# A planned two-layer transformer kernel on one core: weighted values by unit instead of by pair, a one-instruction spread of masked values, one-instruction query scaling, and a newly searched order

## The chip, the cores and the metric

The kernel runs on one core of a Trainium2 chip, as one launch. The metric is the device time of that launch in microseconds, the median of several executions. Times of the profile come from one profiled execution.

## The reference, and what must be computed

Sixteen sequences of 256 tokens with 128 features go through four stages, each followed by a residual and a layer norm. All numbers are 32-bit floats.

```python
x = ln(x + attention(x, Wq, Wkv, Wo, bo))                 # 16 heads of 64, softmax over 256 keys
x = ln(x + routed_ffn(x, signatures, ...))                # a tile of 64 chosen per token, then a tiny spline net
x = ln(x + gate * linear_attn(ln(x)) + (1 - gate) * window_attn(ln(x)) ...)   # window of 65 keys, 16 heads of 8
x = ln(x + moe(causal_qk_norm_attention(ln(x))))          # 16 heads of 64, causal; then 8 experts, all run, 128 -> 512 -> 128
```

Two of the four stages hold an attention with 16 heads of 64. For each head the weights are `softmax(q k^T)` over 256 keys (causal in the second one), and the head's output is `weights @ v`. In the causal attention q and k are divided by their norm and multiplied by a learned scale per feature. The window attention has 16 heads of 8 features; its values `h @ wv_loc + bv_loc` are needed head by head.

## The kernel before: tiling, stages, and who sets the order

**Work units.** The 16 sequences form `NG = 8` groups of two (512 tokens). Every group goes through stages a (first attention), b (routed net), c (linear and window attention), d (causal attention) and e (experts). Within a stage a or d a sequence is worked in *units* of four heads, a unit being two *pairs* of two heads (64 + 64 features fill 128 partitions).

**A pair** (`pair`, from L643) issues: the scores of both heads (64 rows by 128 columns of the array, mode "r", L662 on); a masking add in the causal case (L669); negated row maxima (L678, L688); two exponentials with row sums per head (L707); a reciprocal (L714); a scaling on GpSimd (L720); a transpose of the weights on TensorE into PSUM (L735) and its copy to a `pt` tile on VectorE or ScalarE (L587, L585). Then the weights meet the values, `values`, in a mode of 128 rows by 64 columns ("c64"), so that two heads run side by side into one PSUM bank of which a pair uses 256 columns, and one copy of 128x256 takes the result to an `ov` tile. Four `ov` tiles, one a pair, are multiplied into the width of the model by `into_width`.

**The window attention** (stage c) works in 64 blocks of 64 queries (8 groups, 2 sequences, 4 blocks). Its values are spread into four copies, each zero except for one of every four heads (tiles `vm`, three of them, [128, 4, 128]), by four VectorE additions a block of 4 x 8 columns each (`spread`, L1128). The product with `vm` runs in mode "c32" (128 rows by 32 columns).

**The causal queries** (stage d, `keep`, L1289 on ScalarE, L1291 on VectorE): the projected queries of a unit stand in one PSUM bank of 512 columns, 256 a pair; each pair is scaled by its own column of `qks`, in an instruction of its own, which the planner may give to VectorE or ScalarE.

**Experts** (stage e): per expert four "up" products (128x512, L579), four Gelu activations (L1433), sixteen "down" products in four accumulations, and four accumulating VectorE instructions (L1449). The weights `w1` and `w2` of every expert (256 KB each) are loaded by SyncE's queue again for every group (L1420, L1423), into a pool of two tiles each.

**The order is planned.** No engine's order is written by hand. Every piece above is a task (`W.add`) with allowed engines, a cost in ns, the buffers that it reads, writes or holds, and a due time: `due(g, stage) = g * PACE[stage] + OFF[stage]`, in units of a group. Before the program is emitted, `Plan.line` walks through a list schedule with its own costs: it always takes the task that can begin first, ties broken by due time. Buffers come from the pools of `SLOTS` (class, columns, count); four PSUM banks ("p") and two double banks ("s") are fixed. `SHIFTS` is a list of seeds; each one adds a random disturbance to the due times of some tasks, and the list is what a search kept. The program is then emitted in that order, and each engine runs its own instructions in order and waits on semaphores. When tasks of another array mode follow each other the planner reckons with a drain (`DRAIN`, `CHANGE`), and with 1300 ns when ScalarE changes its function table (`SWITCH`). The Gelus of `NBURST = 2` experts are a *burst*: once ScalarE has begun one, it takes nothing else until the burst is done.

Of the kernel before, what the change touches and what calls it, by code (L numbers as in the profile page):

```python
# [19 lines left out]
P = 128  # L20
# [7 lines left out]
QC = 64  # L28
# [7 lines left out]
NX = 5  # L36
NBURST = 2

OFF = {"a": 0.116, "b": 1.829, "c": 2.055, "d": 3.635, "e": 5.316}
PACE = {"a": 0.877, "b": 0.855, "c": 0.892, "d": 0.951, "e": 0.997}  # L40


def due(g, stage):
# [3 lines left out]

SLOTS = (
    ("x", 512, 5),
    ("xT", 512, 2),  # L50
    ("ua", 512, 5),
    ("uq", 512, 4),
    ("ud", 512, 4),
    ("pb", 512, 5),
    ("pt", 512, 5),
    ("ov", 256, 7),
    ("m", 64, 18),
    ("k1", 256, 6),
    ("b", 512, 2),
    ("sc", 288, 1),  # L60
    ("c", 512, 6),
    ("vl", 516, 1),
    ("qm", 512, 1),
    ("pbC", 512, 2),
    ("ptC", 512, 3),
    ("d", 512, 3),
    ("h2", 512, 1),
    ("kn", 512, 2),
    ("sq", 512, 2),
    ("e", 512, 1),  # L70
    ("hid", 512, 6),
    ("w1", 512, 2),
    ("w2", 512, 2),
)

# [26 lines left out]
class Plan:  # L102
# [11 lines left out]


    SHIFTS = (
        342893, 622819, 786828, 493542, 1031372, 82152, 761358, 224577, 886183, 799202, 814949, 920728, 485348,
        97950, 792974, 882706, 644055, 901515, 175912, 740398, 460392, 490772, 219754, 766672, 812234, 385264,
        789951, 343118, 300004, 391487, 87697, 604865, 1032146, 998679, 152137, 764351, 457160, 307203, 582915,
        594534, 694184, 860491, 449845, 535977, 830298, 828009, 821526, 248210, 581561, 551500, 161509, 113298,  # L120
        555122, 883686, 415166, 991453, 344589, 404904, 418158, 370246, 601370, 461514, 823304, 25842, 794354,
        915253, 557407, 471164, 404291, 181653, 172993, 113307, 463275, 910893, 228032, 531592, 575482, 539031,
        84463, 349997, 228975, 77199, 436200, 405493, 989484, 4908, 562557, 73629, 962183, 941096, 638556,
        301435, 941950, 50702, 302818, 746995, 428703, 741343, 563752, 593640, 707837, 189096, 580269, 586128,
        882519, 591742, 638991, 205226, 680625, 626345, 1043368, 975522, 58852, 258028, 483328, 694436, 909676,
        241425, 473674, 1020055, 78442, 359882, 670620, 772336, 80084, 741629, 7155, 470604, 868845, 984347,
        1018080, 1031109, 71709, 237942, 360624, 360862, 1000988, 139054, 901420, 822374, 801430, 585138,
        797439, 64477, 369282, 125845, 898084, 716005, 751543, 409421,
    )

    def __init__(self, slots):
# [170 lines left out]
def kernel(ctx: ExitStack, tc: tile.TileContext, a: dict, out: bass.AP):  # L302
# [229 lines left out]
    hm = ctile("hm", [P, WH])  # L532

    NVM = 3
    vms = [ctile(f"vm{i}", [P, 4, D]) for i in range(NVM)]

    hsum = ctile("hsum", [P, 2, 32])
    cmask = ctile("cmask", [P, P])
# [97 lines left out]
        else:  # L636
            W.add("V", dve(512), lambda: nc.vector.tensor_scalar(o(), tp(), scale, shift, ALU.mult, ALU.add), r=[tp], w=[o])

    def pair(pi, qT, kT, v, ov, causal, rq, un=0):

# [51 lines left out]
        for par in range(2):  # L695
# [44 lines left out]
            W.add("P", 40 + pe(P, count=ncol // P, passes=1), turn, r=[pb], w=[tps, chain[1]], hold=[pt])  # L740
            W.add("VS", (dve(ncol), scl(ncol)), lambda e, pt=pt, tps=tps: copy(e, pt()[:, :ncol], tps()[:, :ncol]), r=[tps], w=[pt])
            pts.append(pt)
        ops = W.buf("p", "ops")

        def values():
            vv = v("p (k n) -> p k n", k=2)
            for kc in range(2):
                q0 = P if causal and kc else 0
                for par in range(2):
                    hc = slice((2 * pi + par) * DH, (2 * pi + par + 1) * DH)  # L750
                    mm(
                        ops()[par * DH : (par + 1) * DH, q0:S],
                        vv[:, kc, hc],
                        pts[par]()[:, kc * S : kc * S + S - q0],
                        start=kc == 0,
                        stop=kc == 1,
                    )

        W.add("P", pe(ncol, cols=0), values, r=[v] + pts, w=[ops, chain[2]], hold=[ov], mode="c64")
        W.add("VS", (dve(256), scl(256)), lambda e: copy(e, ov(), ops()[:, :S]), r=[ops], w=[ov])  # L760

    def into_width(ovs, w, hf, o, name):

        ps = W.buf("p", "po" + name)
        for qc in range(2):
            def go(qc=qc):
                for i in range(4):
                    mm(
                        ps()[:, qc * P : (qc + 1) * P], ovs[i]()[:, qc * P : (qc + 1) * P], w[:, 4 * hf + i, :],
                        start=i == 0, stop=i == 3,  # L770
                    )

            W.add("P", pe(P, count=4), go, r=ovs, w=[(ps, qc)])
        o(ps)


    def stage_a(g):
# [12 lines left out]
        def unit(b, p2):  # L790

            W.at = base + (4 * b + p2) / 8
            qT, kT, v = W.buf("ua", "qTA"), W.buf("ua", "kTA"), W.buf("ua", "vA")
            ps_q, ps_k, ps_v = W.buf("p", "psq"), W.buf("p", "psk"), W.buf("p", "psv")
            for dst, ps, w, scale in ((qT, ps_q, wq, DH**-0.5), (kT, ps_k, wkv, None)):

                def proj(ps=ps, w=w):
                    for i in range(2):
                        p = 2 * p2 + i
                        mm(ps()[:, i * S : (i + 1) * S], w[:, p * P : (p + 1) * P], xT()[:, b * S : (b + 1) * S])  # L800

                W.add("P", pe(S, count=2), proj, r=[xT], w=[ps], hold=[dst])

                def keep(e, ps=ps, dst=dst, scale=scale):
                    if scale is None:
                        copy(e, dst(), ps())
                    elif e == "S":
                        nc.scalar.mul(dst(), ps(), scale)
                    else:
                        nc.vector.tensor_scalar(dst(), ps(), scale, None, ALU.mult)  # L810

                W.add("SV", (scl(512), dve(512)), keep, r=[ps], w=[dst])

            def proj_v():
                for kc in range(2):
                    c0 = H * DH + p2 * 256
                    mm(ps_v()[:, kc * 256 : (kc + 1) * 256], xT()[:, b * S + kc * P : b * S + (kc + 1) * P], wkv[:, c0 : c0 + 256])

            W.add("P", pe(256, count=2), proj_v, r=[xT], w=[ps_v], hold=[v])
            W.add("SV", (scl(512), dve(512)), lambda e: copy(e, v(), ps_v()), r=[ps_v], w=[v])  # L820
            got = []
            for i in range(2):
                W.at = base + (4 * b + p2 + (i + 1) / 3) / 8
                ov = W.buf("ov", "ovA")
                pair(i, qT, kT, v, ov, False, None)
                got.append(ov)
            return got

        def seq(b):
            for hf in range(2):  # L830
# [184 lines left out]
    def stage_c(g):  # L1015
# [51 lines left out]
        for b in range(2):  # L1067
# [35 lines left out]
            for i, (w0, w1_) in enumerate(win_of):  # L1103
# [19 lines left out]
                W.add("P", pe(P), lambda pvw=pvw, w0=w0, w1_=w1_, nk=nk, b=b: mm(pvw()[:nk, :D], hT()[:, b * S + w0 : b * S + w1_], wvw), r=[hT], w=[pvw, vt])  # L1123

                def spread(pvw=pvw, vm=vm, nk=nk):
                    for l in range(4):
                        own = lambda t: t.rearrange("p (g e) -> p g e", e=4 * WD)[:, :, l * WD : (l + 1) * WD]
                        V.tensor_tensor(out=own(vm[:nk, l, :]), in0=own(pvw()[:nk, :D]), in1=own(bvw[:nk, :]), op=ALU.add)  # L1128

                W.add("V", 394, spread, r=[pvw], w=[vt])  # L1130
                sps = W.buf("s", "spsC")

                def scores(sps=sps, qm=qm, w0=w0, w1_=w1_, nk=nk, b=b):
# [48 lines left out]
                def values(po=po, pts=pts, vm=vm, nk=nk):  # L1182

                    for l in range(4):
                        for j in range(4):
                            r = slice(32 * j, 32 * j + 32)
                            h = 4 * j + l
                            c = ((h // 2) % 4) * P + (h % 2) * QC
                            mm(po()[r, :QC], vm[:nk, l, r], pts[j // 2]()[:nk, c : c + QC], start=l == 0, stop=l == 3)

                W.add("P", 600, values, r=[vt] + pts, w=[po, chain_c[2]], hold=[winT], mode="c32")
                W.add(
# [52 lines left out]
    def stage_d(g):  # L1245
# [9 lines left out]
        def half(b, hf):  # L1255
# [13 lines left out]
            for u in range(2):  # L1269
# [10 lines left out]
                squared = object()  # L1280
                W.add("S", scl(512), lambda sq_q=sq_q, ps_q=ps_q: act(sq_q(), ps_q(), AF.Square), r=[ps_q], w=[sq_q, squared])

                for i in range(2):

                    def keep(e, ps_q=ps_q, qT=qT, u=u, i=i):
                        p = 2 * (2 * hf + u) + i
                        c, o = qks[:, p : p + 1], slice(i * S, (i + 1) * S)
                        if e == "S":
                            A.mul(qT()[:, o], ps_q()[:, o], c)  # L1289
                        else:  # L1290
                            V.tensor_scalar(qT()[:, o], ps_q()[:, o], c, None, ALU.mult)  # L1291

                    W.add("VS", (391, 357), keep, r=[ps_q, squared], w=[(qT, i)])
            pq, nT, pn = W.buf("p", "pq"), W.buf("k1", "nT"), W.buf("p", "pnT")

            def norms():
# [34 lines left out]
            for u in range(2):  # L1331
# [20 lines left out]

                W.add("P", pe(P, count=4, passes=1), turn, r=[kn], w=[tps], hold=[kT])
                W.add("SV", (scl(512), dve(512)), lambda e, kT=kT, tps=tps: copy(e, kT(), tps()), r=[tps], w=[kT])
                for i in range(2):
                    W.at = base + (4 * b + 2 * hf + u + (i + 1) / 3) / 8
                    ov = W.buf("ov", "ovD")
                    pair(i, qTs[u], kT, v, ov, True, rqk, u)
                    got.append(ov)
            return got  # L1360

        def seq(b):
# [148 lines left out]
```

## Time and profile before

| what | value |
|---|---|
| time, median of 3 executions | 2079.08 us (2076.2 to 2080.76) |
| the profiled execution's own time | 2078.85 us |
| its span, first to last instruction | 2077.1 us |
| mean granted TensorE clock | 0.994 |
| ScalarE, copies `ov` of 128x256 | 107, mean 381 ns |
| VectorE, copies `ov` of 128x256 | 149, mean 416 ns |
| VectorE, spread additions | 256, 29.9 us busy in all |
| ScalarE / VectorE, query scalings of 128x256 | 89 of 507 ns / 39 of 478 ns |
| first and last matmul | begin at 5.5 us, end at 2064.9 us |

In the profile, PE is the matmul pipe, PEld its weight loads, DVE is VectorE, ACT ScalarE, POOL GpSimd, SP SyncE. A 32-bit matmul is two passes in the records (a transpose is one), so 9602 matmul instructions are 16394 records. The end of a matmul's record is modelled and lies behind the start of its successor, so the pitch from start to start tells what a matmul costs, not the record's length.

### The profile page before, as it was taken

The numbers are of one execution on the slowest core, as the hardware profiler recorded it, in microseconds if no ns is written. First come the engines' busy times: TensorE is split into PE (matmuls) and PEld (weight loads), VectorE is DVE, ScalarE is ACT, GpSimd is POOL, SyncE is SP. The second block draws the span as 40 slices with busy tenths as digits, with TensorE's granted clock in tenths as the row PEclk, the third lists the DMA queues.
The fourth block names the chain that finished last, engine by engine and source line by source line (L and its number), as shares of the span: only waits on it lengthen the run. The fifth ranks groups of instructions, "written<-read, shape, count | busy, mean of one in ns | idle before, by whom it ended". The sixth has DMA issues, their size and how long they took to land.

```text
span 2077.1 us, 46271 instructions
## 1 busy us (share of the span) xinstructions
PE 2007.3 (97%) x16394; PEld 1524.6 (73%) x16394; DVE 1583.7 (76%) x4843; ACT 1328.9 (64%) x4329; POOL 906.4 (44%) x1552
## 2 busy tenths in 40 slices
PE   8999999999999999999999999999999999999987
PEld 6777777776777777767777777777776776777755
DVE  6888989899936999469994599976897597485442
ACT  3556667777746776567775577763775587486542
POOL 4435565556505545146552265542463263152131
PEclk9999999999999999999999999999999999999989
DMA  6200000000011000110001100001001100100101
GB/s 137 47 1 1 2 2 1 2 2 1 2 57 31 7 1 2 51 33 12 2 2 33 50 12 2 2 21 45 19 7 36 47 7 22 52 16 26 57 21 51
DMA packets 69526, 47.74 MB, mean 23 GB/s; under 512 B 12112, under 2 KB 59952, under 8 KB 69296
## 3 DMA queue, kind: packets, MB, share of 16 engines
q1 hardware_dynamic: 68720, 43.74, 7.7%
q8 instruction: 130, 2.13, 0.4%
q10 hardware_dynamic: 576, 1.05, 0.2%
q14 instruction: 100, 0.82, 0.1%
HBM read 41.89 MB, written 2.88 MB: 22 GB/s over the span
## 4 chain that ended last, share of the span: by engine, by line
PE 60%; DVE 29%; ACT 5%; POOL 3%; issue 2%; DMA 0%; POOLq 0%; DVEq 0%; ACTq 0%; SPq 0%
PE p L579 43%; PE s L579 8%; PE p L735 5%; ACT pb L707 3%; DVE m L678 3%; DVE pt L587 2%; DVE m L688 2%; DVE s L669 2%; PE p L1175 2%; DVE s L1146 1%; DVE m L1151 1%; DVE x L617 1%; DVE m L1324 1%; DVE m L601 1%; PE p L1349 1%
## 5 line engine op out<-in xcount | busy, mean ns | idle before, releaser
L720 POOL TENSOR_SCALAR pb<-pb,m 128x256 f32<-128x256 f32 (+1 forms) x1024 | 461.6, 466 | 560.8 <-DVE m L714 491.4
L1433 ACT ACTIVATE hid<-p,b 128x512 f32<-128x512 f32 x256 | 173.3, 687 | 317.2 <-PE p L579 313.0
L707 ACT ACTIVATE pb<-s,m 128x256 f32<-128x256 f32 x512 | 237.4, 486 | 78.9 <-DVE m L688 71.3
L735 PE MATMUL p<-ident,pb 128*128 128x128 f32 x1792 | 267.5, 279 | 8.3 <-POOL pb L720 2.2
L707 ACT ACTIVATE pb<-s,m,m 128x128 f32<-128x128 f32 (+1 forms) x512 | 256.4, 524 | 22.7 <-DVE m L684 20.2
L579 PEld LDWEIGHTS p<-w,hid 128*128 128x128 f32 x2048 | 239.5, 192 | 25.9 <-issue 20.6
L735 PEld LDWEIGHTS p<-ident,pb 128*128 128x128 f32 x1792 | 201.4, 141 | 76.9 <-POOL pb L720 37.6
L579 PE MATMUL p<-w,hid 128*128 128x128 f32 x2048 | 243.1, 276 | 0.8 <-ACT hid L1433 0.2
L579 PE MATMUL p<-h,w 128*128 128x512 f32 x512 | 240.1, 605 | 0.1
L1449 DVE SCALAR_TENSOR_TENSOR e<-p,m,e 128x128 f32<-128x128 f32 x256 | 74.6, 344 | 206.1 <-PE p L579 155.3
L1169 POOL TENSOR_TENSOR pbC<-pbC,m 128x384 f32<-128x384 f32 (+1 forms) x128 | 119.7, 939 | 166.3 <-DVE m L1165 117.4
L1161 ACT ACTIVATE pbC<-s,m 128x96 f32<-128x96 f32 (+1 forms) x512 | 174.1, 376 | 8.5 <-DVE m L1151 5.4
L587 DVE COPY pt<-p 128x512 f32<-128x512 f32 (+1 forms) x258 | 156.8, 618 | 28.1 <-PE p L735 27.5
L585 ACT COPY pt<-p 128x384 f32<-128x384 f32 (+1 forms) x254 | 131.2, 542 | 70.4 <-PE p L735 64.9
L688 DVE TENSOR_REDUCE m<-s 128x4 f32<-128x1024 f32 x128 | 153.9, 1215 | 10.8 <-PE s L579 9.9
L579 PEld LDWEIGHTS p<-h,w 128*128 128x128 f32 x512 | 91.9, 192 | 93.8 <-issue 79.5
L579 PE MATMUL s<-ua,ua 64*128 64x256 f32 x1024 | 135.5, 391 | 1.9 <-ACT pb L707 1.6
L678 DVE TENSOR_REDUCE m<-s 128x2 f32<-128x256 f32 (+1 forms) x256 | 131.2, 547 | 0.6
L579 PE MATMUL p<-pt,ua 128*64 128x256 f32 x1024 | 130.4, 388 | 0.2 <-DVE m L1312 0.2
L714 DVE RECIPROCAL m<-m 128x2 f32<-128x2 f32 x512 | 78.3, 155 | 61.9 <-ACT pb L707 60.1
L1161 ACT ACTIVATION_READ_ACCUMULATOR pbC<-s,m 128x1 f32 x512 | 117.3, 229 | 0.0
L579 PE MATMUL s<-ud,uq 64*128 64x128 f32 (+1 forms) x1024 | 111.8, 341 | 3.7 <-ACT pb L707 3.3
(268 smaller groups left out, 4325.5 us busy)
## 6 DMA issues: line engine op xcount, KB each, us to landing
w<-in_L_ffn_w_dram SPq DMA_DIRECT2D x128, 256.0 KB, 2.7
x<-_attn_hidden_states_dram SPq DMA_DIRECT2D x8, 256.0 KB, 5.0
out_dram<-x SPq DMA_DIRECT2D x7, 256.0 KB, 2.7
dpad<-k SPq DMA_DIRECT2D x1, 768.0 KB, 9.9
wq<-in_L_attn_Wq_dram ACTq DMA_DIRECT2D x2, 256.0 KB
wkv<-in_L_attn_Wkv_dram ACTq DMA_DIRECT2D x2, 256.0 KB, 5.6
wkv<-in_L_attn_Wkv_dram SPq DMA_DIRECT2D x2, 256.0 KB, 6.3
wo<-in_L_attn_Wo_dram SPq DMA_DIRECT2D x1, 512.0 KB
```

Of the source, the lines that this page charges most:

```text
L579: nc.tensor.matmul(o, lhsT=lhsT, rhs=rhs, start=start, stop=stop)
L585: nc.scalar.copy(o, i)
L587: nc.vector.tensor_copy(o, i)
L678: lambda qc=qc, c0=c0, nk=nk: nc.vector.tensor_reduce(nm()[:, :, qc], sps(S2, a=2)[:, :, c0 : c0 + nk], AX.X, ALU.max, negate=True),
L688: lambda: nc.vector.tensor_reduce(nm(), sps(S2, a=2).rearrange("p a (b k) -> p a b k", k=S), AX.X, ALU.max, negate=True),
L707: act(pb()[:, c0 : c0 + nk], s[:, par, c0 : c0 + nk], AF.Exp, bias=nmx()[:, 2 * par + qc : 2 * par + qc + 1], accum_out=sums()[:, 2 * par ...
L714: W.add("V", 73, lambda par=par: nc.vector.reciprocal(sums()[:, 2 * par : 2 * par + 2], sums()[:, 2 * par : 2 * par + 2]), w=[sm])
L720: eng.tensor_scalar(pb()[:, c0 : c0 + nk], pb()[:, c0 : c0 + nk], sums()[:, 2 * par + qc : 2 * par + qc + 1], 1.0, ALU.mult, ALU.mult,)
L735: nc.tensor.transpose(tps()[:, at * P : (at + 1) * P], pb()[:, c0 + kc * P : c0 + (kc + 1) * P], ident)
L1161: act(pb("p (u k) -> p u k", u=4)[:, u, :nk], s8[:, hp, :nk], AF.Exp, bias=nmx()[:, hp : hp + 1], accum_out=sm()[:, u : u + 1])
L1169: G.tensor_tensor(out=w4, in0=w4, in1=sm()[:, :4].unsqueeze(2).to_broadcast([P, 4, nk]), op=ALU.mult)
L1433: W.add("S", 571, lambda ph=ph, hid=hid, ec=ec: act(hid(), ph(), AF.Gelu_apprx_tanh, bias=b1[:, ec : ec + 1]), r=[ph], w=[hid], table="gel ...
```

## The change

Five things are edited together.

1. `pair` ends with the transposed weights and returns its two `pt` tiles. A new function `weighted` takes the four `pt` tiles of both pairs of a unit, runs the matmuls of both pairs as one task into one full PSUM bank (512 columns), and copies them out with one instruction of 128x512. `ov` tiles are 512 wide (3 of them, where there were 7 of 256), and `into_width` picks its halves.
2. `spread` is one VectorE addition with a strided output of 4 x 4 x 8 columns; the `vm` tiles grow to 4 x 136 columns to allow the stride.
3. `keep` of a causal unit is one task: on VectorE one multiplication of 128x512 by the two columns of `qks`, broadcast; on ScalarE still two instructions of 128x256.
4. The pools of `SLOTS` have other counts.
5. `OFF`, `PACE` and `SHIFTS` are new (173 seeds where there were 150), so every engine's order is another.

```diff
-OFF = {"a": 0.116, "b": 1.829, "c": 2.055, "d": 3.635, "e": 5.316}
-PACE = {"a": 0.877, "b": 0.855, "c": 0.892, "d": 0.951, "e": 0.997}
+OFF = {"a": 0.033, "b": 1.808, "c": 2.055, "d": 3.839, "e": 5.324}
+PACE = {"a": 0.875, "b": 0.807, "c": 0.831, "d": 0.822, "e": 0.923}
...
-    ("xT", 512, 2),
+    ("xT", 512, 1),
...
-    ("pb", 512, 5),
-    ("pt", 512, 5),
-    ("ov", 256, 7),
-    ("m", 64, 18),
-    ("k1", 256, 6),
+    ("pb", 512, 4),
+    ("pt", 512, 7),
+    ("ov", 512, 3),
+    ("m", 64, 14),
+    ("k1", 256, 2),
...
-    ("pbC", 512, 2),
-    ("ptC", 512, 3),
+    ("pbC", 512, 3),
+    ("ptC", 512, 2),
...
-    ("kn", 512, 2),
+    ("kn", 512, 4),
...
-    ("hid", 512, 6),
-    ("w1", 512, 2),
+    ("hid", 512, 9),
+    ("w1", 512, 1),
...
+    def weighted(pts, v, ov, causal):
+        ncol = 3 * P if causal else 4 * P
         ops = W.buf("p", "ops")
         def values():
             vv = v("p (k n) -> p k n", k=2)
-            for kc in range(2):
-                q0 = P if causal and kc else 0
-                for par in range(2):
...
+            for pi in range(2):
+                for kc in range(2):
+                    q0 = P if causal and kc else 0
+                    for par in range(2):
+                        hd = 2 * pi + par
+                        mm(
+                            ops()[par * DH : (par + 1) * DH, pi * S + q0 : (pi + 1) * S],
+                            vv[:, kc, hd * DH : (hd + 1) * DH],
+                            pts[hd]()[:, kc * S : kc * S + S - q0],
+                            start=kc == 0,
+                            stop=kc == 1,
+                        )
-        W.add("P", pe(ncol, cols=0), values, r=[v] + pts, w=[ops, chain[2]], hold=[ov], mode="c64")
-        W.add("VS", (dve(256), scl(256)), lambda e: copy(e, ov(), ops()[:, :S]), r=[ops], w=[ov])
+        W.add("P", 2 * pe(ncol, cols=0), values, r=[v] + pts, w=[ops, chain[2]], hold=[ov], mode="c64")
+        W.add("VS", (dve(512), scl(512)), lambda e: copy(e, ov(), ops()), r=[ops], w=[ov])
...
-                    for l in range(4):
-                        own = lambda t: t.rearrange("p (g e) -> p g e", e=4 * WD)[:, :, l * WD : (l + 1) * WD]
-                        V.tensor_tensor(out=own(vm[:nk, l, :]), in0=own(pvw()[:nk, :D]), in1=own(bvw[:nk, :]), op=ALU.add)
-                W.add("V", 394, spread, r=[pvw], w=[vt])
+                    heads = lambda t: t.rearrange("p (g l e) -> p l g e", g=4, l=4)
+                    own = vm.rearrange("p (l c) -> p l c", l=4)[:nk, :, :D].rearrange("p l (g c) -> p l g c", g=4)[:, :, :, :WD]
+                    V.tensor_tensor(out=own, in0=heads(pvw()[:nk, :D]), in1=heads(bvw[:nk, :]), op=ALU.add)
+                W.add("V", 200, spread, r=[pvw], w=[vt])
...
+                        V.tensor_tensor(
+                            out=qT("p (i t) -> p i t", i=2), in0=ps_q("p (i t) -> p i t", i=2),
+                            in1=qks[:, p : p + 2].unsqueeze(2).to_broadcast([P, 2, S]), op=ALU.mult,
+                        )
-                    W.add("VS", (391, 357), keep, r=[ps_q, squared], w=[(qT, i)])
+                W.add("VS", (dve(512), 714), keep, r=[ps_q, squared], w=[qT])
```

## Prediction

> **What bounds the kernel now.** I read the page's busy times, its slices and its chain first.
>
> ```profile
> span 2077.1 us, 46271 instructions
> PE 2007.3 (97%) x16394; PEld 1524.6 (73%) x16394; DVE 1583.7 (76%) x4843; ACT 1328.9 (64%) x4329; POOL 906.4 (44%) x1552
> ...
> PE   8999999999999999999999999999999999999987
> ...
> PE 60%; DVE 29%; ACT 5%; POOL 3%; issue 2%; DMA 0%; POOLq 0%; DVEq 0%; ACTq 0%; SPq 0%
> ```
>
> PE is busy in every slice; no other engine is. The chain puts 29% on DVE, but that is work which PE happened to wait for last, beside a PE that was elsewhere full. So the time is PE's own work, plus what PE loses between tasks. A modelled end hides the small losses, so I took pitches, from the start of each PE task (2480 of them) to the next. With the shortest pitch of each kind of task, its own work is 1871 us. The order of before changes array mode 744 times, at 0.097 us each (72 us). Pitches above that sum to about 123 us of waits. Ahead of the first matmul lie 5.5 us, behind the last 12.2 us, and the profiled execution, 2078.85 us, adds 1.75 us to the span (it stands 0.2 us under the median of the runs shown).
>
> What a mode run costs is read in the timeline of PE (start, length, what). First a run of two pairs' values, then a run of one pair:
>
> ```profile
> 81.55 1.95 PE L579 MATMUL p<-pt,ua 128*64 128x256 f32 x16
> 83.43 1.13 PE L579 MATMUL p<-xT,wq 128*128 128x256 f32 x4
> ```
>
> ```profile
> 284.06 1.08 PE L579 MATMUL p<-pt,ua 128*64 128x256 f32 x8
> 285.08 1.13 PE L579 MATMUL p<-c,wg 128*128 128x512 f32 x2
> ```
>
> Two pairs together take 83.43 - 81.55 = 1.88 us, one alone 1.02 us. So a run costs 0.15 us beyond its matmuls (2 x 1.02 - 1.88): some 0.10 to empty the array into the next mode and 0.05 to fill it.
>
> The waits of the weight loads name what PE waits for (total us, times, longest):
>
> ```profile
> PEld p L579 <- issue: 158.9, 627, 1.5
> PEld p L735 <- POOL pb L720: 37.6, 110, 1.1
> ...
> PEld s L579 <- ACT pb L707: 15.5, 35, 2.0
> PEld p L1175 <- POOL pbC L1169: 12.3, 25, 1.2
> ```
>
> No single wait stands out: many short ones, spread over all stages (4 to 15 us in every 100, mode changes included), most at the transposes of weights. "issue" is a weight load that had no place to go to; PE mostly works beside it.
>
> **Joined values.** The matmuls are the same 9602. The obvious sum, 128 runs of 0.15 us = 19 us, is wrong: the order of before already puts two pairs' values together in 108 of its 148 runs of this mode, and only 40 stand alone. After has 128 runs, one a unit: 20 fewer, 20 x 0.05 = 1.0 us of fills. All mode changes fall from 744 to 681: 63 x 0.097 = 6.1 us. **Sum -7.1 us**, on PE itself, hidden by nothing. The joined task waits for four `pt` copies where one pair waited for two; the planner sets it later, and whatever is queued behind it on PE would wait too. The values' waits were 5.4 us in 242 waiting tasks; after has half as many. What is late next is `into_width`, which has 1.45 us of PE work ahead of it at the median before and 1.62 after.
>
> **Copies, spread, scaling.** The copies of `ov` go from 149 on DVE and 107 on ACT (416 and 381 ns) to 79 and 49 of 128x512 (rows of that shape: 679 and 598 ns): -8 and -11 us. Spread goes from 256 additions, 29.9 us in all, to 64 of 128 elements; no row has this stride, so I bound it by the 128x64 copy (210 ns) and by four old ones (467 ns), and take the 128x128 copy from PSUM, 277 ns: 18 us, -12. Scaling on DVE goes from 39 x 478 to 14 x 687 ns (row of a 128x512 addition from PSUM): -9; on ACT 100 halves where there were 89, +6. The planner gives DVE 33 more copies of `pt` and some of other tiles, about +31, which ACT loses. DVE and ACT end within 5 us of where they were before table loads. Both are under 80% busy and PE's work lies beside theirs, so I cost this at nothing directly; it counts through PE's waits, next.
>
> **The new order: waits.** This is the large term, and the trace can't show it. I counted, from both orders alone, the *cover* of each PE task that waits on a semaphore: the PE work standing between it and the last PE task on which the awaited instruction depends (through semaphores and the in-order queues). Before's trace gives the mean wait for each class of cover:
>
> | cover, us | tasks before | wait, us | mean | tasks after | at that mean |
> |---|---|---|---|---|---|
> | under 0.9 | 69 | 18.7 | 0.27 | 36 | 9.8 |
> | 0.9 to 1.5 | 282 | 25.0 | 0.089 | 269 | 23.9 |
> | 1.5 to 2.5 | 803 | 43.0 | 0.054 | 700 | 37.5 |
> | 2.5 to 4 | 681 | 23.3 | 0.034 | 687 | 23.5 |
> | over 4 | 409 | 13.1 | 0.032 | 423 | 13.5 |
> | sum | 2244 | 123.2 | | 2115 | 108.2 |
>
> **-15 us.** It is an estimate: cover knows nothing of how long DVE, ACT and POOL take. Below, I bound it by half of what can go: of the 123 us some 45 are bubbles near 0.1 us without a releaser, some 20 stand at the start and where the last group passes from stage d to e (1995 to 2010 us), which after has too; half of the other 60 is -30. Above, by no gain at all, 0.
>
> **Table loads on ACT.** The Gelu bursts of before often ran together. After, they stand apart:
>
> ```profile
> L707 ACT ACT_TABLE_LOAD x16 | 20.5, 1283 | 0.8 <-DVE m L684 0.6
> ...
> L1433 ACT ACT_TABLE_LOAD x13 | 16.7, 1283 | 0.2
> ```
>
> There were 42 loads, 13 of them for the experts' Gelu; after has 64, 24 of them for it. A load takes 1283 ns, and in nearly all places the instruction before it ends 18 ns earlier and the next begins 12 ns later: 1.31 us a switch, 22 x 1.31 = 29 us more of ACT. ACT has room; in the 8 us behind a load for exp PE's waits were 0.66 us against 0.48 at the mean rate, behind one for Gelu 0.58. So 11 more pairs cost about 11 x 0.28 = **+3 us**; bounds 0 and 29.
>
> The Trainium skill speaks against this harder ("ScalarE: Activation LUTs", section What ACT_TABLE_LOAD costs): it gives the same 1283 ns but adds a drain of about 1380 ns, 2.66 us a switch, which would make 59 us of ACT; this trace shows no such drain, gaps of 18 and 12 ns in its place, so the measurement stands.
>
> **One w1 buffer.** The load of an expert's w1 can now begin only when the last up product of the expert before has ended. The shortest such turn in before (start, us, engine):
>
> ```profile
> 1950.38 1.02 PE L579 MATMUL p<-h,w 128*128 128x512 f32 x2
> 1951.43 0.34 SPq L1420 DMA_DIRECT2D w<-in_L_ffn_w_dram  x1
> 1954.18 1.10 PE L579 MATMUL p<-h,w 128*128 128x512 f32 x2
> ```
>
> The up product ends its pitch of 0.86 us at 1951.24, the load is issued 0.19 us later and the next product begins at 1954.18: a turn of 2.94 us. In after 49 first up products depend on such a turn, with covers of 3.57 us at the median, 17 of them under 3.2, one of these 1.78. What they lack of 2.94 us sums to 1.2 us, of 3.3 us to 5.6, of 3.6 to 12. I take **+2 us**; bounds 1 and 12. POOL's instructions and SP's DMAs (212) are the same in number.
>
> **Sum:** 2078.85 - 7.1 - 15 + 3 + 2 = 2061.75, **2062 us**. The tail behind the last matmul is the same code, and the last group's experts again run alone.
>
> **Rivals.**
> *Better cover than priced* (chance 0.13): the other 60 us of waits mostly go, -45 instead of -15: about 2030. For it: short covers halve, the transposes of weights gain 0.23 us of cover at the median, `hid` has nine tiles. Against: the 0.1 us bubbles stay, and DVE is no emptier.
> *The order brings nothing* (0.10): waits stay at 123 us, loads and w1 take back the mode changes: 2078.85 - 7 + 5 = 2077; this is also the case that joining saves nothing much because pairs already stood together.
> *The single w1 buffer decides* (0.15), slower: the load stands behind w2, x or output transfers in SP's queue and the turn grows. It passes before's time from a turn of about 3.9 us on, where the 49 covers lack 24 us; at 4.5 us they lack 52: about 2108. For it: the x loads of the same 256 KB took 5.0 us to land. Against: those fell into the crowded start; w loads took 2.7 us, and DMA is under a fifth busy after the first slices.
> *The forecast* (0.62): 2046 to 2074.
>
> **How the numbers follow.** A measurement of this kernel tells about 0.2% (4 us) from no change. The forecast and better cover are faster, and a few parts in a hundred of the third: 0.78; same 0.07; slower 0.15. The range 2036 to 2086 leaves out some of better cover and of the w1 case, and takes in a third of the loads' upper bound.
>
> **What would show it.** After's PE pitches: 681 mode changes at 0.097 us; 128 value runs of about 1.88 and 1.45 us; waits near 108 us, fewer of them at L735. ACT with 64 loads, DVE near 1585 us. Spread's new row near 0.28 us. The turn of w1 near 3 us, with first up products seldom waiting for a DMA. The prediction is wrong if PE's waits don't fall with the short covers (then cover is no measure of them), if waits gather behind exp after the extra loads, or if first up products wait for w1 by a microsecond each.

## The result, and the profile after

The changed kernel takes **2068.49 us** (median of 4 executions, 2065.75 to 2069.22), the kernel before 2078.96 beside it: ratio 0.9946, 95% interval [0.9933, 0.996]. The profiled execution took 2068.26 us, its span is 2066.5 us: 10.6 us less. Below, a difference between two kernels is the difference of their ratios to the kernel before, times 2079 us; it is known to 3 or 4 us. The page of the changed kernel, with the lines that answer to those shown of before:

```profile
span 2066.5 us, 45955 instructions
...
PE 1991.7 (96%) x16394; PEld 1527.9 (74%) x16394; DVE 1591.3 (77%) x4608; ACT 1333.8 (65%) x4252; POOL 907.4 (44%) x1552
...
PE   8999999999999999999999999999899999999987
...
PE 66%; DVE 26%; issue 3%; ACT 2%; POOL 2%; DMA 0%; POOLq 0%; SPq 0%; DVEq 0%; ACTq 0%
```

The picture is the same: PE full in all slices, and no other engine. PE's busy time fell by 15.6 us, but modelled ends make that a poor measure. By pitches, as in the prediction, the span divides so (the waits are here net of the tasks that ran a little faster than the reference pitch, which is why before has 121 and not 123):

| us | before | after |
|---|---|---|
| up to the first matmul | 5.5 | 4.9 |
| PE's own work | 1855.0 | 1854.8 |
| mode changes at 0.097 | 72.2 (744) | 66.1 (681) |
| fills of the values' runs at 0.05 | 7.4 (148) | 6.4 (128) |
| PE's waits | 120.8 | 117.7 |
| last task and what follows | 16.3 | 16.7 |

The first row is scatter: other runs of the changed order had 5.2 to 5.7 us there. Mode changes and fills give the 7.1 us that were priced. Waits gave 3.1, where 15 less 5 for table loads and `w1` had been reckoned. The waits of the weight loads, as the view sums them (us, times, longest), show how:

```profile
PEld p L583 <- issue: 153.5, 588, 2.4
PEld p L738 <- POOL pb L723: 37.6, 102, 2.0
...
PEld s L583 <- ACT pb L710: 14.8, 36, 2.0
PEld p L1187 <- POOL pbC L1181: 8.3, 14, 2.0
PEld p L1363 <- POOL kn L1353: 8.1, 10, 1.9
```

At the transposes of weights (L738) there are 102 waits instead of 110 and the sum is the same 37.6 us: 0.37 us each instead of 0.34, and the longest is 2.0 us where it was 1.1. The transposes of `kn` have come up: in the same view of before they stand at 1.7 us, 4 times, longest 0.8. By pitch, waits of up to 1 us fell from 95.6 to 86.0 us in all, those over 1 us rose from 28.2 to 36.3.

The new and altered instructions are as priced. Groups of the changed kernel by form (busy us, mean ns, idle before):

```profile
L1302 DVE TENSOR_TENSOR uq<-p,qks 128x512 f32<-128x512 f32 x14 | 9.4, 674 | 0.2 <-ACT sq L1293 0.2
...
L1140 DVE TENSOR_TENSOR vm<-p,bvw 96x128 f32<-96x128 f32 x32 | 8.7, 271 | 0.0
...
L1140 DVE TENSOR_TENSOR vm<-p,bvw 128x128 f32<-128x128 f32 x32 | 8.5, 273 | 0.6 <-PE p L583 0.6
```

The spread takes 272 ns (277 expected), the scaling 674 (687). All 128 runs of values hold two pairs, as here in PE's timeline, where the start of the next task shows 284.89 - 283.01 = 1.88 us:

```profile
283.01 1.95 PE L583 MATMUL p<-pt,ua 128*64 128x256 f32 x16
284.89 2.00 PE L583 MATMUL s<-ua,ua 64*128 64x256 f32 x16
```

### The profile page after: what moved, and what is told of

Same layout as the page of the kernel before. It is cut to its first block, busy times and chain, and to the rows that moved or that the text cites. A ratio compares the mean times of both kernels' runs of the same rounds, so it can differ in the third digit from the quotient of the medians.

```text
span 2066.5 us, 45955 instructions
## 1 busy us (share of the span) xinstructions
PE 1991.7 (96%) x16394; PEld 1527.9 (74%) x16394; DVE 1591.3 (77%) x4608; ACT 1333.8 (65%) x4252; POOL 907.4 (44%) x1552
## 4 chain that ended last, share of the span: by engine, by line
PE 66%; DVE 26%; issue 3%; ACT 2%; POOL 2%; DMA 0%; POOLq 0%; SPq 0%; DVEq 0%; ACTq 0%
PE p L583 47%; PE s L583 9%; PE p L738 7%; DVE m L681 2%; DVE s L1158 2%; DVE s L672 2%; PE p L1187 1%; DVE pt L591 1%; DVE m L1163 1%; DVE m L691 1%; DVE x L621 1%; DVE m L605 1%; ACT pb L710 1%; PE p L1363 1%; DVE ptC L591 1%
## 5 line engine op out<-in xcount | busy, mean ns | idle before, releaser
L738 PE MATMUL p<-ident,pb 128*128 128x128 f32 x1792 | 262.8, 278 | 9.1 <-POOL pb L723 3.2
L738 PEld LDWEIGHTS p<-ident,pb 128*128 128x128 f32 x1792 | 203.5, 141 | 71.7 <-POOL pb L723 37.6
L591 DVE COPY pt<-p 128x512 f32<-128x512 f32 (+1 forms) x291 | 175.8, 617 | 32.3 <-PE p L738 30.5
L589 ACT COPY pt<-p 128x384 f32<-128x384 f32 (+1 forms) x221 | 113.8, 540 | 96.9 <-PE p L738 91.9
L691 DVE TENSOR_REDUCE m<-s 128x4 f32<-128x1024 f32 x128 | 153.5, 1217 | 18.6 <-PE s L583 18.4
L681 DVE TENSOR_REDUCE m<-s 128x2 f32<-128x512 f32 (+1 forms) x256 | 131.1, 546 | 0.6
L583 PE MATMUL p<-pt,ua 128*64 128x256 f32 x1024 | 124.6, 385 | 0.5 <-DVE pt L591 0.5
L583 PEld LDWEIGHTS s<-ua,ua 64*128 64x128 f32 x1024 | 91.3, 186 | 29.4 <-issue 11.1
```

Source lines behind the costliest of these rows:

```text
L583: nc.tensor.matmul(o, lhsT=lhsT, rhs=rhs, start=start, stop=stop)
L589: nc.scalar.copy(o, i)
L591: nc.vector.tensor_copy(o, i)
L681: lambda qc=qc, c0=c0, nk=nk: nc.vector.tensor_reduce(nm()[:, :, qc], sps(S2, a=2)[:, :, c0 : c0 + nk], AX.X, ALU.max, negate=True),
L691: lambda: nc.vector.tensor_reduce(nm(), sps(S2, a=2).rearrange("p a (b k) -> p a b k", k=S), AX.X, ALU.max, negate=True),
L738: nc.tensor.transpose(tps()[:, at * P : (at + 1) * P], pb()[:, c0 + kc * P : c0 + (kc + 1) * P], ident)
```

## The experiments

Four theories stood against each other: that the gain is the mode changes and the new order's cover (the prediction); that the joining alone brings it; that the shorter VectorE instructions bring it; that the order does. Except where an order is said to change, a kernel below keeps that of the kernel it starts from, task by task, and alters what a task issues.

### The vector instructions undone, in the new order

`undo_vector`: the new order, pools and joined values; spread and scaling as before.

```diff
-    V.tensor_tensor(out=own, in0=heads(pvw()[:nk, :D]), in1=heads(bvw[:nk, :]), op=ALU.add)
+    for l in range(4):
+        V.tensor_tensor(out=own[:, l], in0=heads(pvw()[:nk, :D])[:, l], in1=heads(bvw[:nk, :])[:, l], op=ALU.add)
...
-    V.tensor_tensor(out=qT(...), in0=ps_q(...), in1=qks[:, p : p + 2]..., op=ALU.mult)
+    for i in range(2):
+        o = slice(i * S, (i + 1) * S)
+        V.tensor_scalar(qT()[:, o], ps_q()[:, o], qks[:, p + i : p + i + 1], None, ALU.mult)
```

> The changed kernel with its order, costs and pools kept to the task, but the spread again as four VectorE additions a block and the causal scaling on VectorE again as two instructions of 128x256. That puts back about 29.9 - 17.2 = 13 us of VectorE for the spread and 14 x (2 x 478 - 674 ns) = 4 us for the scaling. Theory (PE's own work and the order set the time, VectorE has room): 2068.5 us plus 0 to 3. Rival (the gain came from the relief of VectorE): the 17 us show for the most part, 2076 us or more.

Measured: 2078.58 us, ratio 1.0002 [0.9993, 1.0011], **+11.6 us** over the changed kernel. The whole gain is gone, with mode changes and fills still 7.1 us cheaper than before: PE's waits are 128.0 us, 10.2 more than with the short instructions and 7.2 more than in the kernel before. Then one edit at a time, `undo_spread` (the first half of this diff) and `undo_keep` (the second):

> The changed kernel, its order and its query scaling kept; only the spread is four additions again, 64 times. A set of four took 0.467 us of VectorE and the one addition takes 0.272, so VectorE has 64 x 0.195 = 12.5 us more. Undoing spread and scaling together cost 10 us of time for about 16 us of VectorE. Theory (VectorE's work counts through PE's waits wherever it stands, some 0.6 us of time per us of VectorE): 12.5 x 0.6 = +7.8 us, 2076 us. Rival 1 (the scaling carries it, because ScalarE's square stands ahead of it and the query products behind): 0 to +3 us, 2068 to 2071. Rival 2 (any disturbance of the searched order costs the same, whatever its size): +10 us, 2078.

> The changed kernel, its order and its spread kept; only the 14 query scalings on VectorE are two instructions again: 2 x 0.473 us where one took 0.674, so 14 x 0.272 = 3.8 us more of VectorE. Theory (0.6 us of time per us of VectorE): +2.3 us, 2071 us. Rival 1 (the scaling carries the 10 us): +7 to +10 us, 2075 to 2078. Rival 2 (any disturbance of the searched order costs about the same): +10 us, 2078.

Measured: `undo_spread` 2076.77 us, ratio 0.9986 [0.9977, 0.9995], **+8.3 us**; `undo_keep` 2070.58 us, 0.9959 [0.9945, 0.9972], **+2.7 us**, which alone is within what can be told. They add up to 11.0, and to 11.6 together: the theory's sizes. VectorE's busy time had risen by 10.5 and 3.0 us. It is the spread, 64 instructions shorter by 0.2 us, that carries most of the gain. The loss has no one place: task by task against the changed kernel's profile, PE in `undo_spread` loses 5.4 us behind the first matmul, 33 steps of over 0.15 us adding 11.2 and 17 giving back 7.3, and no kind of task stands for more than 1.5 of it. How the spread's time comes to PE isn't traced further.

### The short spread, in the old order

`spread_before`: the kernel before, with the one-instruction spread and the wider `vm` tile, the planner's cost left as it was, so that every engine's order stays.

> The kernel before, its order kept on every engine (the planner's cost of the spread is left at its old figure); only the 64 spreads are one addition each, into a tile with the wider stride. VectorE has 64 x 0.195 = 12.5 us less. Theory (VectorE's work counts through PE's waits in any order): -7.8 us, about 2070 us against 2078. Rival (the gain lies in the fit of an order to the durations it was searched with; in the old order a shorter instruction only ends earlier and whatever follows waits for something else): 0 to -2 us, 2076 to 2078; a loss if VectorE's earlier finish lets it take something that PE doesn't need first, which its fixed order excludes.

Measured: 2074.42 us, ratio 0.9978 [0.9969, 0.9987], **-4.6 us**, between the theory and its rival. VectorE's busy time fell by 10.7 us, PE's waits by 4.5. So the four corners are:

| ratio to before | long vector instructions | short spread (and scaling, in the new order) |
|---|---|---|
| old order | 1 | 0.9978 [0.9969, 0.9987] |
| new order, joined values | 1.0002 [0.9993, 1.0011] | 0.9946 [0.9933, 0.996] |

Joining, pools and new order alone bring nothing that can be told; the shorter instructions bring 4.6 us in the old order and 11.6 in the new one (8.3 for the spread alone). The spread's 8.3 and 4.6 us lie 3.7 apart, about the error, so that it is worth more in the new order isn't shown. The split can also be read the other way: with the short spread and the old kind of scaling in both, joining and new order bring 4.0 us (`undo_keep`, 0.9959, against 0.9978). The new order was planned with the short spread's cost (200 ns where it was 394), so part of what the spread is worth there may be the fit of an order to its durations.

### Does VectorE's work count anywhere?

Two kernels add 64 reductions of a constant tile, read by nobody, to the changed kernel: `extra_attention` ahead of every eighth reciprocal of the attentions, `extra_experts` ahead of each expert's first accumulation.

```diff
+    if more:
+        nc.vector.tensor_reduce(scr, ident, AX.X, ALU.max)
     nc.vector.reciprocal(sums()[:, 2 * par : 2 * par + 2], sums()[:, 2 * par : 2 * par + 2])
```

> The changed kernel and its order; 64 extra VectorE reductions of a constant 128x128 tile, whose result nothing reads, one in every fourth pair of the attentions, each right ahead of the reciprocal of a pair's first head (between exp and GpSimd's scaling). A record should be near 0.27 us and VectorE some 0.2 us longer each, 12.5 us in all, as much as undoing the spread added (12.5 us, +8.3 us of time). Theory 1 (a us of VectorE counts wherever PE waits for what follows it in the queue): +5 to +9 us, 2073 to 2077. Rival (the spread's place counts, since the window product and its PSUM bank wait for it): 0 to +3 us, 2068 to 2071.

> The changed kernel and its order; the same 64 extra VectorE reductions, but one in each of the 64 experts, right ahead of its first accumulation. There VectorE waited 162 us in all for PE, so an instruction with nothing to wait for slips into that idle time, where the waiting is long enough. Theory 1a (it is not VectorE's work that counts but work which PE's next tasks stand behind): 0 to +3 us, 2068 to 2071. Rival (every us of VectorE counts about the same, wherever it stands): +5 to +9 us, 2073 to 2077.

Measured: `extra_attention` 2072.32 us, ratio 0.9971 [0.9961, 0.9981], **+5.2 us**; `extra_experts` 2069.66 us, 0.9956 [0.9943, 0.997], **+2.1 us**, not to be told from none. VectorE's busy time is up by 5.6 us in the first and by 13.8 in the second, though in both a reduction starts 0.19 us ahead of its successor at the median, 12 us for all 64. So it isn't VectorE's sum that counts: 12 to 14 us more in the experts cost 2, where undoing the spread, 10.5 us, cost 8.3. The same 64 reductions cost 5 in the attentions; but that is only 3.1 us more than in the experts, about the error, and of the 6.3 us that the profiled execution of `extra_attention` lost behind its first matmul 3.6 stand in one stretch, between 960 and 1000 us of the changed kernel. That what stands behind the instruction in the queue decides is argued, not shown.

`keep_on_act` moves the 14 scalings of VectorE to ScalarE, at the same place of the order:

```diff
-    t.fn(e)
+    t.fn("S" if "qks" in t.fn.__code__.co_freevars and t.fn.__name__ == "keep" else e)
```

> The changed kernel and its order; the 14 query scalings of a unit that stand on VectorE are done by ScalarE, at the same place of the order, as two instructions of 128x256 each. VectorE loses 14 x 0.674 = 9.4 us, ScalarE gains 28 x about 0.5 = 14 us. If relief of VectorE paid at the lower of the rates that the runs gave (0.36 us of time per us, from the kernel before with the one-instruction spread), and ScalarE's work cost nothing: -3.4 us, 2065 us, the first version under the changed kernel. Rival (ScalarE's queue holds the exponentials that PE waits for, so its work counts as much as VectorE's): +2 to +6 us, 2070 to 2074.

Measured: 2071.69 us, ratio 0.9959 [0.9945, 0.9972], **+2.7 us**: no gain. VectorE has 5.9 us less, ScalarE 7.9 more, and PE's waits for the exponentials (the third line of the waits shown above) go from 14.8 to 18.6 us; they are 16.5 in `undo_keep` and `extra_experts`, which give ScalarE nothing more to do. Whether ScalarE's work counts as VectorE's does can't be told from +2.7.

### The joining undone on PE

`split_values`: in 124 of the 128 units the two pairs' values are torn apart again, with PE's next task of another mode between them.

```diff
-            for pi in range(2):
+            for pi in which:
...
+                    line = new[: at_ + 1] + [(second, "P", 0, 0)] + new[at_ + 1 :]
```

> The changed kernel with its order kept, but in 124 of the 128 units the next PE task, of another array mode, is put between the two pairs' value products, so that the mode changes rise from 681 to 890 and the runs of values from 128 to 252. Theory (a change of mode is paid on PE in full): 209 x 0.097 + 124 x 0.05 = 26.5 us more, about 2095 us. Rival (PE's waits absorb it, since a longer PE covers more of the other engines' work): under half of that, 2069 to 2081 us.

Measured: 2117.9 us, ratio 1.0193 [1.0179, 1.0207], **+51.4 us**. At the prices read from before, 209 more mode changes at 0.097 and 124 more fills at 0.05 make 26.5 us, as expected; by pitch, PE's waits rose by 22.5 us besides, which neither theory had. Where they come from isn't settled. The timeline shows what standing alone means, 1.02 us a pair (the price that was forecast) with another mode's task between:

```profile
65.99 1.08 PE L583 MATMUL p<-pt,ua 128*64 128x256 f32 x8
67.01 1.13 PE L583 MATMUL s<-ua,ua 64*128 64x256 f32 x8
68.07 1.08 PE L583 MATMUL p<-pt,ua 128*64 128x256 f32 x8
69.08 1.14 PE L583 MATMUL s<-ua,ua 64*128 64x256 f32 x8
```

So joining is worth much to an order that would part the pairs. The order of before parted few.

### What the lists of seeds are worth

`plain_before` and `plain_after`: each kernel with `SHIFTS = ()`, so the planner's own order.

> The kernel before with an empty list of seeds: the planner's own order, no search (due times and pools as they are). 777 mode changes (33 more, +3.2 us), 153 runs of values (+0.3 us), 36 table loads instead of 42. Counted by cover, as in the prediction, waits would go from 124 to 129 us. Theory (cover measures the search's worth): +8.5 us, 2087 us. Rival (the search was worth more than cover sees: it fitted an order to this chip's durations): +20 us or more, 2098 or more.

> The changed kernel with an empty list of seeds. 700 mode changes (19 more, +1.8 us), 128 runs of values as now, 58 table loads instead of 64. By cover, waits would go up by 15 us, to where before's stand. Theory (cover): +17 us, 2085 us, about as long as the kernel before without its seeds. Rival 1 (the changed tasks and instructions carry the gain without any search): 2068 to 2074. Rival 2 (the search was worth far more than cover sees): +25 us or more, 2093 or more.

Measured: `plain_before` 2147.72 us, ratio 1.0331 [1.0317, 1.0345]; `plain_after` 2124.7 us, 1.0221 [1.0207, 1.0235]. The old seeds are worth 68.8 us, the new ones 57.2. PE's waits are 185.7 and 166.3 us. Cover, which had put them at 129 and 124, missed most of it. Without seeds the changed kernel is 22.9 us the faster (27.4 in the profiled executions: mode changes 7.5, fills 1.3, waits 19.4, the last holding tasks, pools, due times and shorter instructions together); the old list had won back more of that than the new one.

### Two costs that were suspected

`one_table_after` computes another activation (Tanh for Gelu, in the routed net and the experts), so that ScalarE loads its table once and not 64 times.

> The changed kernel with the same order, where the Gelus of the experts and of the routed net are computed as Tanh (another function of the same length in the table of exp), so that 63 of the 64 table loads fall away; the output is that of another activation. Prediction's price (0.28 us of PE waits a pair of loads): about 9 us less, 2060. Theory after the result (behind the loads the changed kernel's PE waits no more than elsewhere): 0 to 4 us less. Rival (the loads delay the exponentials and were what took the expected gain away): 15 to 29 us less, 2040 to 2053 us.

Measured: 2065.23 us, ratio 0.9944 [0.9929, 0.9959], **-0.4 us**. ScalarE's busy time fell by 83.3 us, 1.32 us for each of the 63 loads, and nothing that can be told came of it, although the loads stand in the same queue as the exponentials:

```profile
L710 ACT ACT_TABLE_LOAD x27 | 34.6, 1283 | 6.9 <-DVE m L691 6.5
...
L1449 ACT ACT_TABLE_LOAD x24 | 30.8, 1283 | 0.4
```

`root_first` takes the longest wait of the changed kernel, 6.3 us where the last group goes from stage d to e. GpSimd's third affine addition of group 7 stood ahead of the root of the last group's norm; it is moved behind it.

> The changed kernel with one swap: GpSimd's last affine addition of the seventh group's experts (1.26 us), which stands ahead of the last group's second norm's root on GpSimd, and the statistics that depend on it on VectorE, come behind that norm. Theory (the wait at the passage from stage d to e, 6.3 us after against 3.9 before, grew because the root queued behind this addition): the root begins at once when its statistics are there, the wait falls to about 4.9 us and the time by 1.4 us to 2067. Rival (the addition is needed by the experts' start as well, so the wait only moves): no change, 2068.5 us.

Measured: 2069.99 us, ratio 0.9961 [0.9949, 0.9974], **+3.1 us**: no gain. The root began 1.33 us earlier, the transposes of `d` only 0.4 us (1984.74 instead of 1985.14), and the products behind them waited 2.94 us for `h`. The last section says what held `d` up.

Four edits of the changed kernel came out at +2 to +3 us (`undo_keep`, `extra_experts`, `keep_on_act`, `root_first`), all against the same four executions of it. Whether a searched order loses as much by any edit, or these executions were a little short, isn't shown; a share of that size may lie in the 8.3 and 11.6 us too.

Two things weren't tried: two `w1` tiles in the new order, and the joined tasks under the old pools, or the old tasks under the new ones (the planner finds no order there: a unit now holds four `pt` tiles at once).

## Why the prediction was right in the number, and where it was wrong

- **What bounds the kernel: right.** PE's own work is the same within 0.2 us in all kernels that keep an order (1.0 in `plain_after`), so what an edit on another engine did to the span is what it did to PE's waits.
- **Joined values, -7.1 us: right.** 681 mode changes and 128 runs, at the prices read from before; in `split_values` a pair alone took the 1.02 us of its price, though the whole run lost 22.5 us more than the prices make. The rival that pairs already stood together is right too: the term was small for that reason.
- **Copies, spread, scaling, "I cost this at nothing directly; it counts through PE's waits": the step that failed.** The durations were right to 2%. But PE's waits were then estimated from cover alone, which doesn't contain the durations of VectorE, so the 12 us of shorter spreads entered no term of the sum. By `undo_vector` the shorter instructions bring 11.6 us in the new order, which is all that was measured, and by `spread_before` the spread alone brings 4.6 in the old one. "Under 80% busy" was taken for room, but 76% is a mean over the span and says nothing of the moments in which PE waits.
- **The new order's waits, -15 us: wrong.** With the old instructions the new order waits 128.0 us against 120.8: **+7.2**, of the other sign; with the short spread in both it waits 117.7 against 116.3 (`spread_before`), +1.4. Either way nothing of the 15 us came. The counts by cover class follow from the order, but in the changed kernel the mean wait of a class did not hold: under 0.9 us of cover, 36 tasks waited 17.7 us (0.49 each, 0.27 before), and from 2.5 to 4 us, 687 tasks 33.9 us, of which 8 waits over 1 us make 11.0. Among the waits that grew are some behind chains over VectorE and GpSimd: at the transposes of `kn` the weight loads waited 8.1 us for GpSimd where they had waited 1.7. This is the case that the text named as its test: cover is no measure of them.
- **Table loads, +3 us: too much.** The 63 loads behind the first are together worth 0.4 us, within the error of none.
- **One `w1` buffer, +2 us: at most of that size.** By pitch, waits of over 0.15 us ahead of up products sum to 5.6 us, where before had 3.7. Only one of them, 0.75 us in the last group, stands at the load by the timeline; the group's row puts 0.6 us to it in all. No run separates it:

```profile
L583 PE MATMUL p<-h,w 128*128 128x512 f32 x512 | 241.3, 602 | 1.0 <-DMA w<-in_L_ffn_w_dram 0.6
```

- **Two sums that don't close.** The parts of before, 5.5 + 1871 + 72 + 123 + 12.2, make 2083.7 us and not the span's 2077.1; the table above closes, with 1855 us of own work. And the rival's 2108 us for a `w1` turn of 4.5 us seems to leave out the 3 us of table loads: 2059.75 + 52 is 2112. Neither enters the forecast.

The forecast came within 7 us by luck, because two errors had opposite signs: an order that was credited with 15 us and costs 1.4 or 7.2, by the instructions it is compared with, and instructions that were credited with nothing and give 4.6 to 11.6. The rival "the order brings nothing" described the order and missed the instructions.

## What to carry to other kernels

When one engine is full and waits a little everywhere, don't price a shorter instruction on another engine at nothing because that engine's busy share leaves room: here 10 to 11 us of VectorE in the spread were worth 8.3 us of time in one order and 4.6 in another, and 13.8 us more in the experts cost about 2. Ask what stands behind the instruction in its engine's queue; these runs fit that, but don't prove it. A measure of an order that leaves out the other engines' durations tells where waits can come and not how long they are. Before crediting a merged task with saved mode changes, count how often the old order had already put its parts together, and keep the order fixed while undoing one edit: two kernels that completed the four corners of order and instruction told what the trace alone could not.

## What the runs showed of the hardware

Some VectorE instructions are held, by as much as a whole GpSimd instruction at a time, while GpSimd works. The clearest row is the 128x4 multiplication at L687, whose inputs both lie in SBUF (minimum, median and maximum in ns, in the changed kernel):

```profile
L687 DVE TENSOR_TENSOR m<-m,m x128: 124/153/1254, 396.0 to 1958.2; 128x4 f32<-128x4 f32 x128
```

Of its 128, some 90 ran beside no GpSimd instruction, and none of these took over 165 ns; eight stood mostly beside a GpSimd addition of 1.27 us (L1019), with a median of 883. Reductions, reciprocals and copies out of PSUM on VectorE don't change in such company (the 128x1024 reduction takes 1.22 us with and without). In all, some 180 VectorE instructions lost 73 us so in the changed kernel, and 70 in the kernel before, so it isn't what tells the two apart; but it makes single waits jump. In the changed kernel, the VectorE timeline of the last scalings of a norm:

```profile
1454.94 0.42 DVE L591 COPY d<-p 128x256 f32<-128x256 f32 x1 [2.81 <-PE p L583]
1455.28 1.79 DVE L621 TENSOR_SCALAR x<-e,m,m 128x128 f32<-128x128 f32 x3
...
1459.25 0.14 DVE L687 TENSOR_TENSOR m<-m,m 128x4 f32<-128x4 f32 x1
```

and of GpSimd:

```profile
1453.86 1.27 POOL L1019 TENSOR_TENSOR b<-b,beta 128x512 f32<-128x512 f32 x1
1455.21 1.26 POOL L1019 TENSOR_TENSOR b<-b,x 128x512 f32<-128x512 f32 x1
```

The scalings began beside the second addition and were held once. The same place in `undo_spread`, VectorE and then GpSimd:

```profile
1459.49 2.89 DVE L621 TENSOR_SCALAR x<-e,m,m 128x128 f32<-128x128 f32 x3
...
1464.56 0.15 DVE L687 TENSOR_TENSOR m<-m,m 128x4 f32<-128x4 f32 x1
```

```profile
1459.42 1.26 POOL L1019 TENSOR_TENSOR b<-b,beta 128x512 f32<-128x512 f32 x1
1460.77 1.27 POOL L1019 TENSOR_TENSOR b<-b,x 128x512 f32<-128x512 f32 x1
```

Here they began just behind the first addition and were held by both: 2.89 us for 1.79. The exponentials whose scores are masked behind them start that much later, and PE's next scores waited 2.37 us instead of 1.06. The longer spread isn't the reason: `undo_keep`, `extra_experts`, `keep_on_act`, `one_table_after` and `root_first`, which leave the spread alone, hold these three scalings for 2.89 or 2.90 us too, and `undo_keep`, which loses 1.3 us of PE's time here, had gained 1.6 in the 16 us before. So a shift in phase moves a microsecond from one wait to another; what it does to the whole time isn't shown. The same hold kept `d` in `root_first`: the addition moved behind the root ran beside the four scalings of `d`, which took 2.05 us instead of 1.11.

The Trainium skill states this ("SBUF — State Buffer", section SBUF: two separate sides): VectorE and GpSimd share one pair of SBUF ports, which whoever starts first holds for its whole instruction while the other is blocked, VectorE's operations with two SBUF inputs (beside a GpSimd operation that reads SBUF) or in a two-port mode among them. The rows above agree, 153 ns against 883 to 1254.
